# A two-layer kernel whose first layer walks its images in wavefronts: two wavefronts of 8 images against three of 4, 8 and 4

## The chip, the cores and the metric

The kernel runs on one core of one Trainium2 chip. A core has TensorE (PE in the profile, with the loading of its stationary operand shown apart as PEld), VectorE (DVE), ScalarE (ACT), GpSimd (POOL) and SyncE (SP), which here only issues DMAs. ScalarE's own queue issues DMAs too. The metric is the time of one execution on the device in microseconds (us), lower is better; the time given is the median of several executions.

## The reference

The input `x` has 16 images of 64 x 64 positions with 128 channels, in float32. Layer 0 normalises each image by groups of 4 channels (the mean and the variance go over all positions of an image), runs a two-dimensional recurrent cell over it and adds the result to `x`. Layer 1 normalises again, runs a selective scan over the positions forward and backward, and adds that. The change touches layer 0 alone:

```python
def col_step(carry, cols):
    h_l, c_l = carry
    pf0, pf1, pi, po, pc, h_u, c_u = cols          # p* = normalised x @ w* + b*
    f0 = jax.nn.sigmoid(pf0 + h_u @ uf0)
    f1 = jax.nn.sigmoid(pf1 + h_l @ uf1)
    hsum = h_u + h_l
    it = jax.nn.sigmoid(pi + hsum @ ui)
    ot = jax.nn.sigmoid(po + hsum @ uo)
    cp = jnp.tanh(pc + hsum @ uc)
    c = f0 * c_u + f1 * c_l + it * cp
    h = ot * jnp.tanh(c)
    return ((h, c), (h, c))
...
x = x + _L0_conv_ref(_gn(x), ...)
x = x + _L1_conv_ref(_gn(x), ...)
```

A position needs the `h` and `c` of the position above it and of the one to its left. All positions of one anti-diagonal are therefore independent of each other, and a 64 x 64 image has 127 anti-diagonals, with 1, 2, ..., 64, ..., 2, 1 positions.

## The kernel before

**Layer 0 (lines 687 to 853).** Channels lie on the 128 partitions. A wavefront is a set of images that go through their diagonals together: the columns of one step are the positions of the diagonal times the images of the wavefront, so a wavefront of 8 images (`HB`) has 8, 16, ..., 512, ..., 8 columns. There are two wavefronts, images 0 to 7 and 8 to 15.

`statistics(b, q)` (lines 706 to 718) loads a quarter of an image (256 KB, into `xs`, a ring of 4), turns its eight blocks of 128 x 128 with TensorE (line 715) into two PSUM tiles and takes their moments on VectorE (line 716, two instructions); after the fourth quarter line 718 gathers the image's moments. `normal(w)` makes a wavefront's scale and shift from them with `group_norm` (lines 658 to 676): three small matmuls, a few VectorE instructions, a Square and a Sqrt on ScalarE.

One step of a wavefront is three calls. `load(k, w)` (lines 760 to 780) brings the diagonal's positions in by DMAs of up to 128 rows (SyncE's queue, line 767, `xl`, a ring of 8), turns the blocks on TensorE (line 771, `pt`), and applies scale and shift on VectorE (lines 774 and 779, `xn`). `cell` (lines 782 to 814) makes `hs`, the sum of the two neighbours' `h` (line 790), then for each of five gates two matmuls, input weights and recurrent weights (lines 796 and 797), each of which the trace shows as two records; ScalarE takes each gate out of PSUM (line 800); products and sums follow on GpSimd (line 808) and VectorE (809 to 812), one more tanh on ScalarE (813) and the new `h` on VectorE (814). `store` (lines 816 to 831) turns `h` back (line 823, `ph`), adds it to `xl` (lines 826 and 829) and sends the blocks to `x1` by DMAs on ScalarE's queue (line 831).

Buffers: the gates have five PSUM banks (`gate`), the turned blocks and statistics share three (`misc`); the activated gates `a_*` and `hs` have two buffers each, `xn` three.

**The order (lines 833 to 853).** The statistics of the first wavefront's 8 images come first, then `normal(0)`. The second wavefront follows `LATER` diagonals behind the first: the 8 other images have 32 quarters (`rest`), and one quarter is taken at each step, so `LATER` is 34. From then on the steps of the two wavefronts alternate until the first has done its 127 diagonals; the second is alone for the last 34. When the statistics are over, `normal(1)` and the zeroing DMAs of layer 1's `diag` tiles (`clear`, 15 of 256 KB) are issued between steps. At each step the load of the next step is issued ahead of the cell, and the store of the step before behind it. A scheduler orders each engine's instructions from this program; each engine then runs its own list in order, and waits by semaphores.

**Layer 1 (lines 856 on)** starts when layer 0 has let go of its buffers; its order is written out by a planner and is not touched.

Of the kernel before, what the change touches and what calls it, by code (L numbers as in the profile page):

```python
# [8 lines left out]
F32 = mybir.dt.float32  # L9
# [5 lines left out]
P = 128  # L15
B, HH, WW, C = 16, 64, 64, 128
L = HH * WW
# [6 lines left out]
NQ, QP = 2, 64  # L24
# [1 line left out]
NCH = L // T  # L26
PAD = TAPS - 1
NB = T // P
HB = B // 2
GI = P // HB  # L30

# [601 lines left out]
@with_exitstack  # L633
def conv_preact_kernel(ctx: ExitStack, tc: tile.TileContext, a: dict):
    nc = tc.nc
    x, out = a["x"], a["out"]

    const = ctx.enter_context(tc.tile_pool(name="const", bufs=1))
    dram = ctx.enter_context(tc.tile_pool(name="dram", bufs=1, space=DRAM))
    x1 = dram.tile([B * L, C], F32, name="x1")  # L640


    ident = const.tile([P, P], F32, name="ident")
    make_identity(nc, ident)
    eps = const.tile([P, 1], F32, name="eps")
    nc.vector.memset(eps, GN_EPS)

    gavg = const.tile([P, P // GROUP, GROUP], F32, name="gavg")  # L650
    gsum = const.tile([P, P // GROUP], F32, name="gsum")
    nc.vector.tensor_reduce(
        gsum, ident.rearrange("p (g k) -> p g k", k=GROUP), mybir.AxisListType.X, ALU.add
    )
    nc.vector.tensor_scalar_mul(gavg, bc(gsum, 2, GROUP), 1.0 / GROUP)
    gavg = gavg.rearrange("p g k -> p (g k)")

    def group_norm(pool, psum, mv, n, tag, bank="misc"):
# [12 lines left out]
        nc.scalar.activation(std, pv, AF.Sqrt, bias=eps)  # L671
        scale = pool.tile([P, n], F32, name=f"scale_{tag}", tag="gn_scale")
        nc.vector.reciprocal(scale, std)
        shift = pool.tile([P, n], F32, name=f"shift_{tag}", tag="gn_shift")
        nc.vector.scalar_tensor_tensor(shift, mean, -1.0, scale, ALU.mult, ALU.mult)
        return scale, shift


    n = max(sum(k in "NU" for k in kinds) for kinds in KINDS)
    diags = [  # L680
        [dram.tile([P, T], F32, name=f"diag_{i}_{k}") for k in range(n)] for i in range(SETS)
    ]
    layer0(tc, a, const, ident, group_norm, x, x1, sum(diags, []))
    layer1(tc, a, const, ident, group_norm, x1, out, diags)


def layer0(tc, a, const, ident, group_norm, x, x1, clear):
# [3 lines left out]
    nc = tc.nc  # L691
    gates = ["f0", "f1", "i", "o", "c"]
    with ExitStack() as ctx:
        wp = ctx.enter_context(tc.tile_pool(name="l0w", bufs=1))
# [7 lines left out]
        NQ = L // P // SB  # L702
# [25 lines left out]
        norm = {}  # L728

        def normal(w):  # L730
            norm[w] = group_norm(gp, psum, mv[:, w * HB : (w + 1) * HB, :], HB, f"l0_{w}")

        for b in range(HB):
            for q in range(NQ):
                statistics(b, q)
        normal(0)
        rest = [(b, q) for b in range(HB, B) for q in range(NQ)]

        state = {}
        for w in range(2):
            for s in "hc":
                for par in range(2):
                    t = wp.tile([P, HH + 1, HB], F32, name=f"{s}_{w}_{par}")
                    nc.vector.memset(t, 0.0)
                    state[s, w, par] = t

        def rows_of(t, w, k, i, m):

            return bass.AP(
                t.tensor,
                t.offset + w * HB * L * C + i * (WW - 1) * C + k * C,
                [[(WW - 1) * C, m], [L * C, HB], [1, C]],
            )

        def blocks_of(n):
            return [(g, min(GI, n - g * GI)) for g in range(-(-n // GI))]

        def load(k, w):  # L760

            lo, hi = max(0, k - (WW - 1)), min(HH - 1, k)
            n = hi - lo + 1
            nm = f"{k}_{w}"
            xl = xp.tile([P, T // P, C], F32, name=f"xl_{nm}", tag="xl")
            for g, m in blocks_of(n):
                nc.sync.dma_start(xl[: m * HB, g, :], rows_of(x, w, k, lo + g * GI, m))
            pt = psum.tile([P, T], F32, name=f"pt_{nm}", tag="misc")
            for g, m in blocks_of(n):
                r = m * HB  # L770
                nc.tensor.transpose(pt[:, g * P : g * P + r], xl[:r, g, :], ident[:r, :r])
            xn = gp.tile([P, HH, HB], F32, name=f"xn_{nm}", tag="xn", bufs=3)
            xv = xn[:, :n, :]
            nc.vector.tensor_mul(
                xv,
                pt[:, : n * HB].rearrange("p (i b) -> p i b", b=HB),
                bc(norm[w][0], 1, n),
            )
            nc.vector.tensor_add(xv, xv, bc(norm[w][1], 1, n))
            return k, w, lo, n, nm, xl, xv  # L780

        def cell(loaded):

            k, w, lo, n, nm, _, xv = loaded
            cols = n * HB
            hp, cp = state["h", w, (k + 1) % 2], state["c", w, (k + 1) % 2]
            hn, cn = state["h", w, k % 2], state["c", w, k % 2]
            up, left = slice(lo, lo + n), slice(lo + 1, lo + 1 + n)
            hs = gp.tile([P, HH, HB], F32, name=f"hs_{nm}", tag="hs")
            nc.vector.tensor_add(hs[:, :n, :], hp[:, up, :], hp[:, left, :])  # L790
            rec = [hp[:, up, :], hp[:, left, :]] + [hs[:, :n, :]] * 3
            act = []
            for gi, g in enumerate(gates):
                pg = psum.tile([P, T], F32, name=f"pg_{g}_{nm}", tag="gate", bufs=5)
                pgv = pg[:, :cols]
                nc.tensor.matmul(pgv, lhsT=w_sb[:, gi, :], rhs=xv, start=True, stop=False)
                nc.tensor.matmul(pgv, lhsT=u_sb[:, gi, :], rhs=rec[gi], start=False, stop=True)
                ag = gp.tile([P, HH, HB], F32, name=f"a_{g}_{nm}", tag=f"a_{g}")
                agv = ag[:, :n, :]
                nc.scalar.activation(  # L800
                    agv.rearrange("p i b -> p (i b)"),
                    pgv,
                    AF.Tanh if g == "c" else AF.Sigmoid,
                    bias=b_sb[:, gi : gi + 1],
                )
                act.append(agv)
# [9 lines left out]
        def store(loaded):  # L816

            k, w, lo, n, nm, xl, _ = loaded
            hv = state["h", w, k % 2][:, lo + 1 : lo + 1 + n, :].rearrange("p i b -> p (i b)")
            ph = psum.tile([P, T // P, C], F32, name=f"ph_{nm}", tag="misc")  # L820
            for g, m in blocks_of(n):
                r = m * HB
                nc.tensor.transpose(ph[:r, g, :], hv[:, g * P : g * P + r], ident)
            full = n // GI
            if full:
                nc.vector.tensor_add(xl[:, :full, :], ph[:, :full, :], xl[:, :full, :])
            if n % GI:
                r = (n % GI) * HB
                nc.vector.tensor_add(xl[:r, full, :], ph[:r, full, :], xl[:r, full, :])
            for g, m in blocks_of(n):  # L830
                nc.scalar.dma_start(rows_of(x1, w, k, lo + g * GI, m), xl[: m * HB, g, :])

        LATER = len(rest) + 2
        ND = HH + WW - 1
        steps = []
        for t in range(ND + LATER):
            steps += [(t, 0)] * (t < ND) + [(t - LATER, 1)] * (t >= LATER)
        before, now = None, load(*steps[0])
        for n in range(len(steps)):
            if rest:  # L840
                statistics(*rest.pop(0))
            elif 1 not in norm:
                normal(1)
                zeros = xp.tile([P, T], F32, name="zeros", tag="xs", bufs=4)
                nc.vector.memset(zeros, 0.0)
            elif clear:
                nc.sync.dma_start(clear.pop(), zeros)
            after = load(*steps[n + 1]) if n + 1 < len(steps) else None
            cell(now)
            if before:  # L850
                store(before)
            before, now = now, after
# [522 lines left out]
```

## Time and profile before

| what | value |
|---|---|
| median of 3 executions | 13241.79 us (13238.22 to 13249.65) |
| the profiled execution, its own time | 13204.66 us |
| its span | 13202.9 us |
| granted TensorE clock, mean over the span | 0.994 |
| PE busy over the span | 12892.4 us (98%) |
| DVE busy over the span | 12069.2 us (91%) |
| ACT busy over the span | 11514.2 us (87%) |
| first gate matmul of layer 0 starts at | 81.30 us |
| last `h` of layer 0 written at | 1548.56 us |

The profiled execution is 37 us shorter than the median of the others. A span is the time from the first to the last instruction of the profiled execution. Matmuls are pipelined and the ends of their records are modelled, so records overlap and a sum of their durations is more than the time they take: what a matmul costs TensorE is read from the distance of two starts. Issuing a DMA is not counted as busy, though it takes time on the queue of the engine that issues it (ACTq, SPq in a timeline). Layer 0 is the first 1549 us of the span, an eighth of it.

### The profile page before, as it was taken

The page shows a single profiled execution, that of the slowest core. Times are in us where ns is not written, and L with a number is a line of the kernel's source. Part 1 is how long each engine was busy: PE and PEld are TensorE (multiplying, and loading weights), DVE is VectorE, ACT ScalarE, POOL GpSimd, SP SyncE. Part 2 cuts the span into 40 slices and gives each one's busy share as a digit, 9 for nine tenths or more (in the row PEclk, how much of TensorE's full clock was granted, in tenths as well). Part 3 has the DMA queues.
Part 4 walks back from the last instruction along what each step waited for, and adds up shares of the span by engine and source line. Part 5 has one row for each costly group of instructions (what it writes and reads, how often), then busy time and mean ns, then how long its engine had stood idle before and what let it go on. Part 6 is the DMA issues. An engine that isn't in the chain of part 4 may idle for free. (4 is left out here: it accounts for less than half of the span.)

```text
span 13202.9 us, 263832 instructions
## 1 busy us (share of the span) xinstructions
PE 12892.4 (98%) x91444; PEld 10824.2 (82%) x91444; DVE 12069.2 (91%) x14353; ACT 11514.2 (87%) x21184; POOL 11263.7 (85%) x4996
## 2 busy tenths in 40 slices
PE   8999899999999999999999999999999999999999
PEld 7666788888888888888888888888888888888887
DVE  6676599999999999999999999999999999999999
ACT  3444599999999999999999999999999999999998
POOL 0111299999999999999999999999999999999999
PEclk8999999999999999999999999999999999999999
DMA  4221266656666666666566666666565656666665
GB/s 143 54 57 52 62 167 163 171 160 171 164 166 165 165 167 162 170 160 172 158 172 162 167 166 164 166 162 171 159 173 161 168 161 170 164 162 166 163 166 146
DMA packets 2777751, 2025.28 MB, mean 153 GB/s; under 512 B 1584848, under 2 KB 1930464, under 8 KB 2776416
## 3 DMA queue, kind: packets, MB, share of 16 engines
q1 hardware_dynamic: 2698464, 1973.16, 56.9%
q10 hardware_dynamic: 77952, 35.24, 1.1%
q8 instruction: 725, 11.88, 0.4%
q14 instruction: 610, 5.00, 0.1%
HBM read 1849.24 MB, written 157.02 MB: 152 GB/s over the span
## 5 line engine op out<-in xcount | busy, mean ns | idle before, releaser
L1221 POOL TENSOR_TENSOR hc<-hst,cr 128x1024 f32<-128x1024 f32 x3328 | 7802.1, 2377 | 286.9 <-DVE hst L1195 226.2
L1195 DVE TENSOR_TENSOR_SCAN hst<-das,carry,hps 128x512 f32<-128x512 f32 x3808 | 4668.2, 1262 | 184.0 <-PE hps L1183 87.2
L1230 PE MATMUL py<-ident,hc 128*128 128x128 f32 x32768 | 4144.9, 274 | 54.8 <-POOL hc L1221 53.4
L1230 PEld LDWEIGHTS py<-ident,hc 128*128 128x128 f32 x32768 | 3672.2, 141 | 450.2 <-issue 272.0
L1145 ACT ACTIVATE das<-dt,A_log_sb 128x512 f32<-128x512 f32 x5888 | 3875.6, 713 | 121.1 <-DVE hst L1195 79.1
L1157 ACT ACTIVATE dbt<-dtxt,bt 128x256 f32<-128x256 f32 x7680 | 3231.7, 498 | 160.0 <-PE hps L1183 147.6
L1150 POOL TENSOR_TENSOR dbx<-dtx,br 128x1024 f32<-128x1024 f32 x1152 | 2728.6, 2382 | 10.1
L1195 DVE TENSOR_TENSOR_SCAN hst<-da,carry,dbx 128x512 f32<-128x512 f32 x2016 | 2469.2, 1261 | 31.7 <-ACT da L1145 29.9
L1183 PE MATMUL hps<-ident,dbt 128*128 128x128 f32 x15360 | 2261.3, 274 | 104.4 <-DVE hc L1223 80.4
L1174 PE MATMUL hps<-dg,dtxt 128*128 128x128 f32 x16384 | 2176.4, 277 | 37.3 <-DVE hst L1195 20.3
L1183 PEld LDWEIGHTS hps<-ident,dbt 128*128 128x128 f32 x15360 | 1782.0, 141 | 434.0 <-issue 300.4
L1174 PEld LDWEIGHTS hps<-dg,dtxt 128*128 128x128 f32 x16384 | 2005.8, 192 | 117.4 <-DVE hst L1195 46.5
L1014 PE MATMUL pp<-xT,wk 128*128 128x512 f32 x4096 | 1901.6, 596 | 1.9 <-ACT xT L984 1.9
L1195 DVE TENSOR_TENSOR_SCAN hps<-das,carry,hps 128x512 f32<-128x512 f32 x1344 | 1654.7, 1266 | 19.2 <-PE hps L1174 9.6
L1145 ACT ACTIVATE da<-dt,A_log_sb 128x512 f32<-128x512 f32 x2304 | 1556.4, 683 | 80.5 <-DVE hst L1195 59.3
L808 POOL TENSOR_TENSOR a_f<-a_f,c 128x288 f32<-128x288 f32 (+40 forms) x254 | 212.0, 835 | 1332.8 <-ACT a_f L800 1261.9
L1223 DVE TENSOR_TENSOR hc<-hps,cr 128x512 f32<-128x512 f32 x1536 | 1025.7, 674 | 225.8 <-DMA cr<-rows 214.2
L1014 PEld LDWEIGHTS pp<-xT,wk 128*128 128x128 f32 x4096 | 716.5, 190 | 628.9 <-issue 604.0
L1119 POOL TENSOR_TENSOR dtx<-dt,xc 128x1024 f32<-128x1024 f32 x256 | 607.7, 2374 | 296.5 <-ACT dt L1113 225.9
L1195 DVE TENSOR_TENSOR_SCAN hst<-das,hps 128x512 f32<-128x512 f32 x544 | 641.7, 1203 | 83.0 <-issue 27.4
L800 ACT ACTIVATE a_f<-pg_f,b_sb 128x288 f32<-128x288 f32 (+40 forms) x508 | 217.0, 471 | 362.5 <-DMA x<-xl 160.1
L1102 PE MATMUL pv<-dbl,dt_wT 128*128 128x256 f32 x2048 | 507.2, 380 | 8.5 <-ACT xc L1025 8.5
(113 smaller groups left out, 12661.8 us busy)
## 6 DMA issues: line engine op xcount, KB each, us to landing
cr<-rows SPq DMA_DIRECT2D x4096, 256.0 KB
br<-rows SPq DMA_DIRECT2D x1152, 256.0 KB
dg<-diag SPq DMA_DIRECT2D x1024, 256.0 KB
yf<-yo SPq DMA_DIRECT2D x128, 512.0 KB
yl<-yf SPq DMA_DIRECT2D x128, 512.0 KB
carry<-hst SPq DMA_DIRECT2D x3328, 1.0 KB
xs<-in_x_dram SPq DMA_DIRECT2D x64, 512.0 KB
xl<-x SPq DMA_DIRECT2D x128, 256.0 KB
```

The source lines that it names most:

```text
L1014: nc.tensor.matmul(self.ps["conv", h], lhsT=wk[:, k, h * P : (h + 1) * P], rhs=xT[self.b % 2][:, t0 : t0 + T], start=(k == 0), stop=(k == ...
L1102: nc.tensor.matmul(pv[:, q * TQ : (q + 1) * TQ], lhsT=dt_wT[:, q, h * P : (h + 1) * P], rhs=self.dbl, start=True, stop=True,)
L1119: nc.gpsimd.tensor_mul(self.dtx, self.dt, self.xc)
L1145: nc.scalar.activation(t, self.dt[:, h, :], AF.Exp, scale=amat[:, h, s : s + 1])
L1150: nc.gpsimd.tensor_mul(t, self.dtx, bc(self.brow.pop(s), 1, NH))
L1157: nc.scalar.activation(t[:, j, :], self.dtxt[:, j, :], AF.Copy, scale=self.bt[:, j, s : s + 1])
L1174: nc.tensor.matmul(t[:, j * P : (j + 1) * P], lhsT=self.dtxt[:, j, h * P : (h + 1) * P], rhs=self.dbt[s][:, j, :], start=True, stop=True,)
L1183: nc.tensor.transpose(t[:, j * P : (j + 1) * P], self.dbt[s][:, j, h * P : (h + 1) * P], ident)
L1195: nc.vector.tensor_tensor_scan(t[:, self.rev], self.da.pop((s, h))[:, self.rev], dbx[:, self.rev], 0.0 if self.first else carry[:, self.d, ...
L1221: nc.gpsimd.tensor_mul(self.hc[s], self.hst[s], bc(self.crow[s], 1, NH))
L1223: nc.vector.tensor_mul(self.hc[s][:, h, :], self.h[s, h], self.crow[s])
L1230: nc.tensor.matmul(self.py[:, j, cols], start=j not in self.banks, stop=last, skip_group_check=True, **how,)
```

## The change

The two wavefronts of 8 images become three, of 4, 8 and 4 images (`WAVES`), whose first images are 0, 4 and 12. Everything that went by `HB` goes by the wavefront's own number of images `nb`; a block of 128 rows holds 32 positions of a 4-image wavefront and 16 of an 8-image one. The statistics of the first 4 images come ahead of the first diagonal. Those of the other 12 (48 quarters) are taken two at each step of the first wavefront (`PACE`), and `normal(w)` follows as soon as a wavefront's last quarter has been taken. The second wavefront starts 18 diagonals behind the first (32 quarters by two, and two more), the third 26. The rings of `scale` and `shift` get three buffers, since three wavefronts' values live at once. The `clear` DMAs are issued after the last quarter, as before.

```diff
-HB = B // 2
-GI = P // HB
+WAVES = ((0, 4), (4, 8), (12, 4))
...
         def normal(w):
-            norm[w] = group_norm(gp, psum, mv[:, w * HB : (w + 1) * HB, :], HB, f"l0_{w}")
-
-        for b in range(HB):
+            b, nb = WAVES[w]
+            norm[w] = group_norm(gp, psum, mv[:, b : b + nb, :], nb, f"l0_{w}")
+
+        for b in range(WAVES[0][1]):
             for q in range(NQ):
                 statistics(b, q)
         normal(0)
-        rest = [(b, q) for b in range(HB, B) for q in range(NQ)]
+        rest = [(b, q) for b in range(WAVES[0][1], B) for q in range(NQ)]
...
-        LATER = len(rest) + 2
+        PACE = 2
+        later = [0]
+        for b, nb in WAVES[1:]:
+            later.append(-(-(b + nb - WAVES[0][1]) * NQ // PACE) + 2)
         ND = HH + WW - 1
-        steps = []
-        for t in range(ND + LATER):
-            steps += [(t, 0)] * (t < ND) + [(t - LATER, 1)] * (t >= LATER)
+        steps = [
+            (t - d, w)
+            for t in range(ND + later[-1])
+            for w, d in enumerate(later)
+            if 0 <= t - d < ND
+        ]
+        zeros = None
         before, now = None, load(*steps[0])
         for n in range(len(steps)):
-            if rest:
-                statistics(*rest.pop(0))
-            elif 1 not in norm:
-                normal(1)
+            if rest and steps[n][1] == 0:
+                for _ in range(min(PACE, len(rest))):
+                    b, q = rest.pop(0)
+                    statistics(b, q)
+                    for w, (first, nb) in enumerate(WAVES):
+                        if (b, q) == (first + nb - 1, NQ - 1):
+                            normal(w)
+            elif not rest and zeros is None:
                 zeros = xp.tile([P, T], F32, name="zeros", tag="xs", bufs=4)
                 nc.vector.memset(zeros, 0.0)
-            elif clear:
+            elif clear and zeros is not None:
                 nc.sync.dma_start(clear.pop(), zeros)
             after = load(*steps[n + 1]) if n + 1 < len(steps) else None
             cell(now)
```

The rest of the diff puts `nb` for `HB` and `gi = P // nb` for `GI` in `rows_of`, `blocks_of`, `load`, `cell`, `store` and the tiles of `h` and `c`.

More of the change, by code (lines that the diff above doesn't have):

```diff
@@ L671, in group_norm @@
         nc.scalar.activation(std, pv, AF.Sqrt, bias=eps)
-        scale = pool.tile([P, n], F32, name=f"scale_{tag}", tag="gn_scale")
+        scale = pool.tile([P, n], F32, name=f"scale_{tag}", tag="gn_scale", bufs=3)
         nc.vector.reciprocal(scale, std)
-        shift = pool.tile([P, n], F32, name=f"shift_{tag}", tag="gn_shift")
+        shift = pool.tile([P, n], F32, name=f"shift_{tag}", tag="gn_shift", bufs=3)
         nc.vector.scalar_tensor_tensor(shift, mean, -1.0, scale, ALU.mult, ALU.mult)
@@ L736, in layer0 @@
         normal(0)
-        rest = [(b, q) for b in range(HB, B) for q in range(NQ)]
+        rest = [(b, q) for b in range(WAVES[0][1], B) for q in range(NQ)]
         state = {}
-        for w in range(2):
+        for w, (_, nb) in enumerate(WAVES):
             for s in "hc":
                 for par in range(2):
-                    t = wp.tile([P, HH + 1, HB], F32, name=f"{s}_{w}_{par}")
+                    t = wp.tile([P, HH + 1, nb], F32, name=f"{s}_{w}_{par}")
                     nc.vector.memset(t, 0.0)
@@ L749, in rows_of, with blocks_of @@
         def rows_of(t, w, k, i, m):
+            b, nb = WAVES[w]
             return bass.AP(
                 t.tensor,
-                t.offset + w * HB * L * C + i * (WW - 1) * C + k * C,
-                [[(WW - 1) * C, m], [L * C, HB], [1, C]],
-            )
-        def blocks_of(n):
-            return [(g, min(GI, n - g * GI)) for g in range(-(-n // GI))]
+                t.offset + b * L * C + i * (WW - 1) * C + k * C,
+                [[(WW - 1) * C, m], [L * C, nb], [1, C]],
+            )
+        def blocks_of(n, gi):
+            return [(g, min(gi, n - g * gi)) for g in range(-(-n // gi))]
         def load(k, w):
             lo, hi = max(0, k - (WW - 1)), min(HH - 1, k)
-            n = hi - lo + 1
+            n, nb = hi - lo + 1, WAVES[w][1]
+            gi = P // nb
             nm = f"{k}_{w}"
             xl = xp.tile([P, T // P, C], F32, name=f"xl_{nm}", tag="xl")
-            for g, m in blocks_of(n):
-                nc.sync.dma_start(xl[: m * HB, g, :], rows_of(x, w, k, lo + g * GI, m))
+            for g, m in blocks_of(n, gi):
+                nc.sync.dma_start(xl[: m * nb, g, :], rows_of(x, w, k, lo + g * gi, m))
             pt = psum.tile([P, T], F32, name=f"pt_{nm}", tag="misc")
-            for g, m in blocks_of(n):
-                r = m * HB
+            for g, m in blocks_of(n, gi):
+                r = m * nb
                 nc.tensor.transpose(pt[:, g * P : g * P + r], xl[:r, g, :], ident[:r, :r])
-            xn = gp.tile([P, HH, HB], F32, name=f"xn_{nm}", tag="xn", bufs=3)
+            xn = gp.tile([P, HH, nb], F32, name=f"xn_{nm}", tag="xn", bufs=3)
             xv = xn[:, :n, :]
@@ L775, in load @@
                 xv,
-                pt[:, : n * HB].rearrange("p (i b) -> p i b", b=HB),
+                pt[:, : n * nb].rearrange("p (i b) -> p i b", b=nb),
                 bc(norm[w][0], 1, n),
@@ L784, in cell @@
             k, w, lo, n, nm, _, xv = loaded
-            cols = n * HB
+            nb = WAVES[w][1]
+            cols = n * nb
             hp, cp = state["h", w, (k + 1) % 2], state["c", w, (k + 1) % 2]
@@ L788, in cell @@
             up, left = slice(lo, lo + n), slice(lo + 1, lo + 1 + n)
-            hs = gp.tile([P, HH, HB], F32, name=f"hs_{nm}", tag="hs")
+            hs = gp.tile([P, HH, nb], F32, name=f"hs_{nm}", tag="hs")
             nc.vector.tensor_add(hs[:, :n, :], hp[:, up, :], hp[:, left, :])
@@ L797, in cell @@
                 nc.tensor.matmul(pgv, lhsT=u_sb[:, gi, :], rhs=rec[gi], start=False, stop=True)
[L798 removed]
+                ag = gp.tile([P, HH, nb], F32, name=f"a_{g}_{nm}", tag=f"a_{g}")
                 agv = ag[:, :n, :]
@@ L818, in store @@
             k, w, lo, n, nm, xl, _ = loaded
+            nb = WAVES[w][1]
+            gi = P // nb
             hv = state["h", w, k % 2][:, lo + 1 : lo + 1 + n, :].rearrange("p i b -> p (i b)")
             ph = psum.tile([P, T // P, C], F32, name=f"ph_{nm}", tag="misc")
-            for g, m in blocks_of(n):
-                r = m * HB
+            for g, m in blocks_of(n, gi):
+                r = m * nb
                 nc.tensor.transpose(ph[:r, g, :], hv[:, g * P : g * P + r], ident)
-            full = n // GI
+            full = n // gi
@@ L825, in store @@
             if full:
                 nc.vector.tensor_add(xl[:, :full, :], ph[:, :full, :], xl[:, :full, :])
-            if n % GI:
-                r = (n % GI) * HB
+            if n % gi:
+                r = (n % gi) * nb
                 nc.vector.tensor_add(xl[:r, full, :], ph[:r, full, :], xl[:r, full, :])
-            for g, m in blocks_of(n):
-                nc.scalar.dma_start(rows_of(x1, w, k, lo + g * GI, m), xl[: m * HB, g, :])
-        LATER = len(rest) + 2
-        ND = HH + WW - 1
@@ L835, in layer0 @@
-        steps = []
-        for t in range(ND + LATER):
-            steps += [(t, 0)] * (t < ND) + [(t - LATER, 1)] * (t >= LATER)
+            for g, m in blocks_of(n, gi):
+                nc.scalar.dma_start(rows_of(x1, w, k, lo + g * gi, m), xl[: m * nb, g, :])
+        PACE = 2
+        later = [0]
+        for b, nb in WAVES[1:]:
+            later.append(-(-(b + nb - WAVES[0][1]) * NQ // PACE) + 2)
+        ND = HH + WW - 1
+        steps = [
[4 more added lines that the diff above has]
+        ]
```

## The prediction

> **What bounds the kernel now.** Only layer 0 changes, so I read it by stages. I took the busy time by windows first: statistics ahead of the first gate, wavefront 0 alone, both wavefronts, wavefront 1 alone. Columns: window, its length, then busy time and records of PE, PEld, DVE, ACT, POOL, then granted clock, DMA share, GB/s.
>
> ```profile
> 0.00:49.00 49.00, 28.16 (x159) 25.17 (x160) 30.48 (x54) 1.28 (x1) 0.70 (x6) 0.83 0.75 251
> 49.00:81.00 32.00, 19.49 (x118) 16.24 (x117) 20.54 (x40) 2.65 (x4) 0.00 (x0) 0.80 0.73 252
> 81.00:261.00 180.00, 176.27 (x1069) 160.47 (x1067) 126.16 (x400) 71.90 (x214) 17.17 (x35) 0.86 0.43 133
> 261.00:1385.00 1124.00, 1116.45 (x4715) 737.39 (x4716) 783.13 (x1797) 497.43 (x1103) 177.72 (x184) 1.00 0.20 53
> 1385.00:1549.00 164.00, 140.53 (x815) 124.86 (x813) 92.43 (x342) 68.69 (x213) 17.14 (x35) 0.90 0.11 29
> ...
> 30.00:40.00 10.00, 5.96 (x46) 4.90 (x47) 7.08 (x12) 0.00 (x0) 0.00 (x0) 1.00 0.88 312
> ...
> 81.00:133.00 52.00, 52.00 (x245) 49.51 (x244) 22.42 (x87) 13.80 (x49) 2.08 (x8) 0.50 0.29 88
> ...
> 1519.00:1549.00 30.00, 28.59 (x135) 27.63 (x134) 9.72 (x62) 10.91 (x40) 1.55 (x7) 0.50 0.02 6
> ```
>
> The pairs (1124 us) keep PE full at full clock. The clock is half in the first diagonals and the last ones, where steps have few columns. Then the price of a gate matmul, from a timeline of PE: starts, durations, shapes.
>
> ```profile
> 1362.23 0.68 PE L796 MATMUL pg_o<-xn,w_sb 128*128 128x304 f32 x2
> 1362.75 0.67 PE L797 MATMUL pg_o<-hs,u_sb 128*128 128x304 f32 x2
> 1363.26 0.68 PE L796 MATMUL pg_c<-xn,w_sb 128*128 128x304 f32 x2
> ...
> 1364.88 0.40 PE L796 MATMUL pg_f<-xn,w_sb 128*128 128x24 f32 x2
> ...
> 1366.92 0.38 PE L797 MATMUL pg_c<-hs,u_sb 128*128 128x24 f32 x2
> 1367.14 1.24 PE L796 MATMUL pg_f<-xn,w_sb 128*128 128x296 f32 x4
> ```
>
> Two records of 304 columns start 0.515 us apart from the next two: 0.257 a record, 0.00084 us a column. All 20 records of a 24-column step take 1364.88 to 1367.14, 2.26 us: 0.113 a record, not 0.020. So a step costs PE 20 x max(0.113, 0.00084 x columns), flat below 134 columns, plus 0.109 for each 128-wide transpose (eight from 138.28 to 139.16). At half clock the floor doubles:
>
> ```profile
> 97.66 1.95 PE L715 MATMUL ps<-ident,xs 128*128 128x128 f32 x8
> ...
> 101.09 0.61 PE L796 MATMUL pg_o<-xn,w_sb 128*128 128x32 f32 x2
> 101.52 0.61 PE L796 MATMUL pg_c<-xn,w_sb 128*128 128x32 f32 x2
> ```
>
> That is 0.213 a record. Last the in-order engines beside PE:
>
> ```profile
> 300.15 0.47 DVE L774 TENSOR_TENSOR xn<-pt,scale_l 128x320 f32<-128x320 f32 x1
> 304.46 2.13 ACTq L831 DMA_DIRECT2D x<-xl  x3
> 304.54 0.19 DVE L774 TENSOR_TENSOR xn<-pt,scale_l 128x48 f32<-128x48 f32 x1
> 306.64 0.94 ACT L800 ACTIVATE a_f<-pg_f,b_sb 128x320 f32<-128x320 f32 x2 [3.40 <-DMA x<-xl]
> ```
>
> A VectorE instruction has some 0.14 us whatever its columns, and a store's issue holds ScalarE's queue 0.7 us; gates stand behind it.
>
> **The change part by part.**
>
> *Fewer statistics first.* The eighth image's gathering (line 718) ends at 75.27, the fourth's at 43.62 (starts 74.90 and 43.25, 0.37 each). The first gate follows 6.03 later, at 81.30: the small matmuls, a Square, a Sqrt and two table loads of 1.28. So it starts at 43.62 + 6.03 = **49.65**, 31.65 earlier.
>
> *PE work by 4-image steps.* A wavefront of 8: 32 diagonals (n up to 16) at the floor, 32 x 2.26 = 72.3; the others hold 4096 - 272 = 3824 positions x 8 x 0.0168 = 513.9; 586 in all. A wavefront of 4: 66 diagonals at the floor = 149.2; 4096 - 1122 = 2974 x 4 x 0.0168 = 199.8; 349. Two of these in place of one of 8: **+112**. Blocks: 316 each for 8 images, 190 for 4; 64 more, load and store at 0.109: +14. Statistics inside the diagonals: 48 quarters for 32, 16 x 8 x 0.109 = +14, the counterpart of the 31.65.
> So PE's need after the first gate is now 2 x 586.3 + 632 x 2 x 0.109 + 27.9 = 1338 of 1467 us elapsed: 129 lost. It becomes 586.3 + 698.0 + 151.7 + 41.9 = 1478. With the start at 49.65 the need alone ends at 1527.5. **The change wins only if its losses stay under 21 us.** I go through them by stage.
>
> *Wavefront 0 alone, diagonals 0 to 17 (4 to 72 columns), 16 statistics transposes a step.* Half clock: the step from 99.79 to 106.28 (6.49) plus 8 x 0.213 = 8.2. Full clock: the step from 139.24 to 142.87 (3.63, with VectorE near full) plus two moments of 0.69 = 5.0. All cold 148, all warm 90. Before, the clock came at 133, eight steps in. A 4-image step has half the columns, which speaks for later; 16 transposes in a row (3.4 us at half clock) for earlier, since with transposes alone on PE the clock was 1.00 from 30 to 40 us. I take eight cold and ten warm: **116**.
>
> *Diagonals 18 to 25, two wavefronts.* Need 39.6 + 12 x 8 x 0.109 = 50; all cold 8 x 9.4 + 6 x 3.4 = 96. I take **60**, nearer the need, as one step has 76 columns or more.
>
> *Diagonals 26 to 126, three wavefronts.* Need, summed by the prices above: 676 in the wide part (56 to 99), 566 in the two narrow parts. The trace gives what is lost on top: the pairs of diagonals 62 to 104 ran 611.2 us (558.65 to 1169.85) for a need of 597.4, factor 1.023; those of 35 to 54 ran 202.9 for 189.0, 1.075. Narrow diagonals are where the fixed parts count: at diagonal 40 (164, 184 and 60 columns) PE needs 9.2, VectorE about 30 x 0.14 + 408 x 0.0098 = 8.2, ScalarE 18 x 0.16 + 408 x 0.0046 + 5 x 0.7 = 8.3 (starts 0.405 apart at 320 columns, 0.19 at 40). Three engines within a tenth, in fixed order and with two `a_*` buffers, where the slack is only the third wavefront's. I take the measured factors: 676 x 1.023 + 566 x 1.075 = **1300**; bounds 1.02 throughout (1267) and 1.25 in the narrow parts (1400).
>
> *Diagonals 127 to 144, wavefronts 1 and 2.* Need 89.8. In the tail of before the clock went at 1519, between steps of 64 and 56 columns that took 3.3 us, with 0.0168 x 60 / 3.3 = 0.3 of the time streaming. Here a pair takes about 5.0 and gets there when its columns sum to some 100, at diagonal 139. Until then 60.1 x 1.1 = 66; six cold pairs of 40 x 0.213 + 4 x 0.213 = 9.4: 56. **122**; all warm 99.
>
> *Diagonals 145 to 152, wavefront 2 alone (32 to 4 columns).* Cold like 1519 to 1549, where 6.5 steps took 30: 8 x 4.6 = **37**.
>
> *At nothing.* The third `normal` with its table loads lies in wavefront 0's lone stretch, where ScalarE is busy 72 of 180; uncovered some 6. On SP two `xs` loads a step now stand ahead of the `xl` loads; they wait for their ring of 4, two steps back, at 512 KB in 5 to 8 us against 251 GB/s in the first window; uncovered, a quarter's 4.2 us (issued 0.73, first transposed 5.0) a step, up to 75. The 15 clears move, DMA share 0.20. State tiles hold the same bytes. Layer 1 has the same list.
>
> *Sum.* 49.65 + 116 + 60 + 1300 + 122 + 37 = 1685 against 1549: **+136 us** on the profiled execution's 13204.7, whose median neighbours are 37 longer: 13241.8 + 136, about 13375.
>
> [...]
>
> **Rivals.**
> - *The clock stays down longer.* Lone stretch 148, two-wavefront stretch 96, ten cold pairs at the end (+18): 86 more, 13461. For it: 52 us at 0.50 with PE full. Against: the bursts of transposes.
> - *ScalarE or VectorE sets the narrow diagonals.* Factor 1.25: +100, 13475. For it: the 3.40 us idle behind a store's issue. Against: 1.075 with two wavefronts, and a third step now lies between a cell and its successor.
> - *Losses nearly vanish*, since three wavefronts cover every chain: 90 + 52 + 1267 + 99 + 37 + 49.65 = 1595, 13288. Against: nothing covers the clock.
> - *The floor isn't a price* (the other side): a step's 20 short records overlap other wavefronts' work, so that 4-image steps go by columns: 0.0168 x 4 x 4096 x 2 = 551 instead of 698 is 147 less than the forecast, and with the losses of the rival before it 13288 - 147 = 13141. It decides once over two thirds of the 147 and the smaller losses come. Against: in the 24-column step PE never idled between records and still took 0.113.
>
> **How the numbers follow.** Forecast 0.62 (its own range 13320 to 13425), clock 0.10, ScalarE or VectorE 0.10, losses vanish 0.12, no floor 0.06. The range 13285 to 13460 leaves out the floor rival and the far ends of two others. A measurement of this kernel tells 0.2%, 26 us, from no change: faster means under 13215, the floor rival; same takes a slice of the vanishing losses, 0.06; slower the rest.
>
> **What would show it.** In the profile after: first gate near 50 us; 20 records of any step under 134 columns in 2.26 us; clock 0.50 for about 65 us from there; 1300 us from diagonal 26 to 126, PE at 9s; clock 0.50 again for the last 90 us; layer 1's span unchanged within 15 us. I am wrong if short records come closer than 0.11 us, if the clock is up from the first step, or if PE idles by over a tenth in the narrow diagonals.

## The result, and the profile after

The changed kernel takes 13380.33 us (median of 4, 13372.76 to 13384.13) against 13245.72 before: a ratio of 1.0102, 95% interval 1.009 to 1.0114. The forecast was 13375, with a range of 13285 to 13460. In the profiled executions layer 0's last `h` is written at 1693.6 us, against 1548.6 before. What comes after it, layer 1, takes 11682 us against 11654, 28 us more where the forecast allowed 15. A second profile of the same changed kernel, on another chip, has 11648, and the other kernels below have 11643 to 11661, so I take that difference for one of executions or chips and not of the change. The two profiled executions are 173 us apart and the medians 135, since the profiled execution of before was the one that lay 37 us under its median.

The same view by windows as before, at the bounds of the stages: ahead of the first gate, wavefront 0 alone, two wavefronts, three wavefronts (diagonals 26 to 55, 56 to 99, 100 to 126), wavefronts 1 and 2 until the clock falls, and the rest of layer 0. Columns are the window, its length, the busy time and records of PE, PEld, DVE, ACT and POOL, then the granted clock, DMA share and GB/s.

```profile
0.00:51.00 51.00, 28.91 (x151) 24.93 (x151) 29.72 (x60) 4.32 (x5) 0.70 (x6) 0.88 0.73 239
51.00:144.00 93.00, 91.55 (x688) 88.27 (x688) 68.84 (x241) 31.23 (x112) 4.77 (x18) 0.85 0.65 207
144.00:200.00 56.00, 54.88 (x441) 51.86 (x438) 40.23 (x171) 27.56 (x98) 5.95 (x16) 0.94 0.49 165
200.00:507.00 307.00, 305.99 (x2087) 283.59 (x2087) 220.36 (x855) 166.75 (x540) 44.37 (x90) 0.97 0.16 44
507.00:1226.00 719.00, 704.34 (x3307) 520.57 (x3308) 511.83 (x1312) 335.58 (x797) 100.52 (x132) 1.00 0.19 54
1226.00:1537.00 311.00, 307.69 (x1904) 266.61 (x1902) 216.90 (x776) 159.21 (x485) 42.58 (x81) 0.98 0.15 43
1537.00:1605.00 68.00, 67.14 (x572) 64.22 (x571) 47.57 (x234) 38.52 (x154) 10.05 (x25) 1.00 0.13 35
1605.00:1694.00 89.00, 87.60 (x406) 83.33 (x405) 27.60 (x171) 29.25 (x114) 4.66 (x19) 0.50 0.02 6
```

The reader is to see three things. PE is full nearly everywhere: the time was not lost to waiting engines, it went into PE. The clock is up for most of the first lone stretch (0.85, against 0.50 in the 52 us after the first gate of before), and down at the end. And the widest part, where only PE's columns should count, has idle PE time: 704 busy of 719.

The price of a short step, in PE's timeline of the changed kernel:

```profile
1367.71 0.43 PE L799 MATMUL pg_f<-xn,w_sb 128*128 128x64 f32 x2
1367.98 0.39 PE L800 MATMUL pg_f<-h,u_sb 128*128 128x64 f32 x2
...
1369.54 0.39 PE L799 MATMUL pg_c<-xn,w_sb 128*128 128x64 f32 x2
1369.76 0.39 PE L800 MATMUL pg_c<-hs,u_sb 128*128 128x64 f32 x2
1370.10 0.41 PE L828 MATMUL ph<-ident,h 128*128 128x128 f32 x2
```

Each pair of records starts some 0.22 us behind the pair before it, also with two other wavefronts' work on either side: a 64-column step takes as long as one of 24 columns did.

Stage by stage, in us; the column "again" is a second profile of the same kernel, on another chip. "Need" counts the records in the trace, each at max(0.113, 0.00084 x columns) for a gate and 0.109 for a transpose, at full clock.

| stage | forecast | measured | again | need |
|---|---|---|---|---|
| first gate at | 49.65 | 51.2 | 49.1 | |
| wavefront 0 alone, diagonals 0 to 17 | 116 | 93.1 | 86.3 | 76 |
| two wavefronts, 18 to 25 | 60 | 55.9 | 58.6 | 49 |
| three, 26 to 55 | 305 | 306.7 | 306.5 | 283 |
| three, 56 to 99 | 692 | 719.3 | 719.3 | 677 |
| three, 100 to 126 | 304 | 311.3 | 312.0 | 282 |
| two, 127 to 144 | 122 | 117.7 | 117.9 | 90 |
| wavefront 2 alone, 145 to 152 | 37 | 38.4 | 38.4 | 20 |
| last `h` of layer 0 at | 1685 | 1693.6 | 1688.0 | |

### The profile page after: what moved, and what is told of

Read it like the earlier page. It is cut to its first block, busy times and chain, and to the rows that moved or that the text cites. A ratio compares the mean times of both kernels' runs of the same rounds, so it can differ in the third digit from the quotient of the medians.

```text
span 13375.9 us, 272473 instructions
## 1 busy us (share of the span) xinstructions
PE 13062.7 (98%) x94118; PEld 11144.4 (83%) x94118; DVE 12179.4 (91%) x15537; ACT 11664.9 (87%) x21951; POOL 11266.8 (84%) x5123
## 5 line engine op out<-in xcount | busy, mean ns | idle before, releaser
L1247 PE MATMUL py<-ident,hc 128*128 128x128 f32 x32768 | 4146.8, 274 | 58.6 <-POOL hc L1238 57.4
L1212 DVE TENSOR_TENSOR_SCAN hps<-das,carry,hps 128x512 f32<-128x512 f32 x1344 | 1654.4, 1265 | 19.8 <-PE hps L1191 9.8
L811 POOL TENSOR_TENSOR a_f<-a_f,c 128x4 f32<-128x4 f32 (+35 forms) x381 | 212.9, 559 | 1477.0 <-ACT a_f L803 1306.8
L803 ACT ACTIVATE a_f<-pg_f,b_sb 128x4 f32<-128x4 f32 (+35 forms) x762 | 289.0, 400 | 383.4 <-PE pg_f L800 171.0
```

The source lines that it names most:

```text
L1212: nc.vector.tensor_tensor_scan(t[:, self.rev], self.da.pop((s, h))[:, self.rev], dbx[:, self.rev], 0.0 if self.first else carry[:, self.d, ...
L1247: nc.tensor.matmul(self.py[:, j, cols], start=j not in self.banks, stop=last, skip_group_check=True, **how,)
```

## The experiments

Eleven kernels ran on three more chips, each beside the kernel before on the same chip; the kernel before had medians of 13207, 13205 and 13208 us there, some 39 us under the first chip's. So ratios and the stages of the traces are compared, not times across chips. A ratio is to the kernel before. In diffs the changed kernel is the other side, if nothing else is said.

**The changed kernel once more.** No edit.

> The changed kernel itself once more, beside the others on one chip, since chips differ by some tens of us in the time of the same kernel. About 1.010 of the time before; layer 0 ends between 1685 and 1705 us, the lone stretch of 18 diagonals takes some 93 us, or, if the clock there is a matter of chance, up to 125.

13350.29 us, ratio 1.0111 (1.0097 to 1.0125). The stages are in the table; the lone stretch differs most (86 and 93 us), by the clock: 0.94 here, 0.85 there.

**Four wavefronts of 4 images: the suspected cost once more.**

```diff
-WAVES = ((0, 4), (4, 8), (12, 4))
+WAVES = ((0, 4), (4, 4), (8, 4), (12, 4))
```

(and four buffers for `scale` and `shift`)

> Four wavefronts of 4 images, leads 0, 10, 18 and 26, so the same start and the same end as the changed kernel, with the 8-image wavefront split once more. Doubles the suspected cost. Theory (PE's floor): PE's need from the first gate on rises from 1436 to 1562 us without the statistics, so layer 0 ends 115 to 140 us later, about 13505, with all steps under 134 columns at 2.26 us for 20 records. Rival (fixed parts of VectorE and ScalarE): 127 steps more at some 10 x 0.15 us on VectorE, 190 us more, about 13570, and PE idle between steps.

13625.16 us, ratio 1.0318 (1.0304 to 1.0332): twice the loss forecast. Its windows, with the same columns:

```profile
47.00:275.00 228.00, 224.11 (x1489) 214.34 (x1487) 134.25 (x560) 87.24 (x310) 13.81 (x50) 0.76 0.40 128
275.00:664.00 389.00, 376.01 (x2731) 351.32 (x2729) 259.37 (x1124) 203.54 (x724) 53.67 (x120) 0.94 0.13 37
664.00:1373.00 709.00, 704.17 (x4212) 663.93 (x4212) 556.29 (x1752) 375.98 (x1058) 112.85 (x176) 1.00 0.19 54
1373.00:1703.00 330.00, 326.01 (x2457) 307.74 (x2456) 230.40 (x1014) 185.66 (x648) 46.88 (x108) 0.96 0.14 38
1703.00:1959.00 256.00, 254.61 (x1185) 242.09 (x1185) 82.89 (x486) 87.54 (x325) 15.12 (x54) 0.51 0.04 10
```

The records' need is 1603 us against 1477 in the changed kernel, +126, as worked out. But from the first gate to the last `h` it takes 1911.4 against 1642.3, +269. The rest is the clock. Its half-clock time is the sum of 2 x (1 - clock) x length: here 109 + 47 + 0 + 26 + 251 = 433 us; in the changed kernel's windows above, from the first gate on, 28 + 7 + 18 + 0 + 12 + 0 + 89 = 154. If half clock doubles the need (a short gate record starts 0.213 us behind the one before at half clock and 0.112 at full clock, medians of both main profiles), half the difference, 140, is what it added; 126 + 140 = 266. The time that neither explains is 88 us in the changed kernel and 92 here, with 127 steps more, so fixed parts of VectorE and ScalarE did not set the pace: the rival, with 190 us for them, falls, although the time lies nearer its 13570 than the theory's 13505. Where the theory fell short is the clock: it counted the floor alone, 126 us, and with 127 steps more the half-clock time rose by 279 us besides.

By the same count, need, half of the half-clock time and the rest, the kernel before has 1337, 46 and 84 us of its 1467.3 from the first gate to the last `h`, and the changed kernel 1477, 77 and 88 of its 1642.3. So the 145 us by which layer 0 ends later are 140 of need, 31 of half clock and 4 of the rest, less the 30 by which it starts earlier.

**Two wavefronts of 8 images, two quarters a step.**

```diff
-WAVES = ((0, 4), (4, 8), (12, 4))
+WAVES = ((0, 8), (8, 8))
```

> The changed kernel with two wavefronts of 8 images again, the statistics still two quarters a step, so the second wavefront starts 18 diagonals behind the first and not 34. Theory (PE's floor of 0.113 us a record is what three wavefronts pay for): without 4-image steps the work falls back to that of before, and the lone stretches shrink from 34 diagonals to 18. First gate near 81, 18 lone steps in some 82 us, pairs 1220 us of need x 1.037 = 1265, lone tail 74 us as in the rows of before from 1474.84 to 1548.56: layer 0 ends near 1502, that is some 190 us under the changed kernel and 45 under the one before, about 13200. Rival (the split into three is what lets PE run full, and only the pace of the statistics and fixed parts of ScalarE and VectorE cost time): pairs 18 apart run into each other's chains, and the time stays at or over 13245.

13170.30 us, ratio 0.9972 (0.9961 to 0.9982): 37 us under the kernel before, and by ratio some 180 under the changed one. Wavefront 0 alone, the pairs, wavefront 1 alone:

```profile
76.00:162.00 86.00, 82.60 (x645) 78.07 (x645) 68.39 (x228) 32.79 (x111) 6.34 (x18) 0.92 0.69 229
162.00:1430.00 1268.00, 1262.63 (x5550) 874.79 (x5547) 901.28 (x2140) 581.33 (x1311) 182.09 (x219) 1.00 0.20 53
1430.00:1504.00 74.00, 62.37 (x398) 58.94 (x397) 34.48 (x168) 29.80 (x111) 6.23 (x18) 0.79 0.06 16
```

86 for an expected 82, 1268 for 1265, 74 for 74; layer 0 ends at 1504.3 for 1502. The pace of the statistics and the shorter lead, here changed together, are worth having; the 4-image wavefronts are what costs: with the same pace the changed kernel takes 214 us more from first gate to last `h`, 140 of them need, 49 half clock and 25 the rest.

**One quarter a step: the pace alone undone.**

```diff
-        PACE = 2
+        PACE = 1
```

> The three wavefronts with one quarter of statistics a step as before, so leads of 34 and 50 diagonals. Undoes the pace alone. Theory (bursts of 16 transposes bring the clock up in the lone stretch, bursts of 8 do not until the steps have some 64 columns): the first 16 steps or so stay at half clock and take 6.4 us each, 100 us, the next 18 about 3.8; with the same need of PE elsewhere and a longer pair stretch and lone tail layer 0 ends 50 to 100 us later than the changed kernel, near 13420. Rival (the clock came up for another reason, the shorter steps): lone steps at 3.7 us from the second on, and the end within 35 us of the changed kernel.

13396.92 us, ratio 1.0145 (1.0131 to 1.0159), 47 us over the changed kernel on this chip; layer 0 ends at 1743.4 against 1688.0, 55 later, as the theory had it (the 18 lone steps behind the cold ones took 4.5 us each, not 3.8). The lone stretch of 34 diagonals in two windows, and a step in it:

```profile
47.00:162.00 115.00, 115.00 (x540) 109.33 (x539) 50.64 (x197) 30.33 (x109) 4.80 (x18) 0.50 0.29 89
162.00:231.00 69.00, 61.94 (x491) 58.32 (x489) 53.34 (x184) 30.19 (x100) 6.56 (x16) 0.95 0.48 147
...
101.86 1.95 PE L714 MATMUL ps<-ident,xs 128*128 128x128 f32 x8
...
104.87 0.63 PE L799 MATMUL pg_i<-xn,w_sb 128*128 128x40 f32 x2
105.30 0.63 PE L799 MATMUL pg_o<-xn,w_sb 128*128 128x40 f32 x2
```

115 us at half clock, PE full: with eight transposes in a row among such short steps the clock stayed at 0.50, and it came when the steps had some 72 columns, as before the change. In the changed kernel it was up before the steps had 24:

```profile
72.48 2.80 PE L714 MATMUL ps<-ident,xs 128*128 128x128 f32 x12
...
75.79 0.42 PE L799 MATMUL pg_i<-xn,w_sb 128*128 128x20 f32 x2
76.05 0.38 PE L799 MATMUL pg_o<-xn,w_sb 128*128 128x20 f32 x2
```

Twelve transposes in one piece, and the gates behind them start at full clock's 0.23 to 0.26 us a pair. So it was with the pace of two, with pieces of 11 to 16 transposes, that the clock came up early: 1.00 from 75.9 to 127.0 us, where that of one had 0.50.

**The store a step later.** This asks where the wide part's 719 us went. Each step's store, whose first part is PE's transposes of `h`, is put behind the gates of the second step after it and not the first:

```diff
-        before, now = None, load(*steps[0])
+        waiting, now = [], load(*steps[0])
...
+            while waiting and waiting[0][1] == now[1] and waiting[0][0] == now[0] - 2:
+                store(waiting.pop(0))
             cell(now)
-            if before:
-                store(before)
-            before, now = now, after
-        store(before)
+            while len(waiting) > 1:
+                store(waiting.pop(0))
+            waiting.append(now)
+            now = after
+        for one in waiting:
+            store(one)
```

> The changed kernel with each step's store issued one step later, so that the transposes of h follow the gates of the second step behind it and not the first. Theory (in the wide diagonals PE waits in front of the transposes of the 8-image wavefront's h, because only a short 4-image step lies between): the gaps in front of these transposes, 31 us from 507 to 1537 us, go nearly all, 20 to 30 us less, about 13355. Rival (VectorE or ScalarE sets the pace there and PE's gap is only where it shows): the gap moves to the gates, time within 8 us of the changed kernel.

13333.79 us, ratio 1.0092 (1.0079 to 1.0105): by ratio 25 us under the changed kernel, within the theory's 20 to 30, but as the sum of two opposite differences. The wide part went from 719 to 692 us, and the lone stretch from 93 to 125. The two windows:

```profile
50.00:175.00 125.00, 124.18 (x689) 118.83 (x690) 70.27 (x241) 31.28 (x111) 4.77 (x18) 0.61 0.51 155
546.00:1238.00 692.00, 691.91 (x3304) 523.39 (x3304) 507.20 (x1309) 332.66 (x793) 102.16 (x132) 1.00 0.20 56
```

The clock was 0.61 in the lone stretch, against 0.85 and 0.94 in the changed kernel; the new order also split the transposes there, into pieces of at most 10 from 60 to 140 us, where the changed kernel has one of 11 or more in nearly every step. The time of this kernel varies: the five executions went from 13302 to 13348 us, and the profiled one is the longest, with a mean clock of 0.988 over the whole kernel where the two shortest have 0.991 and 0.992. To keep the two apart, the next kernel stores later only from diagonal 26 on (the diff is against the kernel just shown):

```diff
-            while len(waiting) > 1:
+            while len(waiting) > (steps[n][0] + later[steps[n][1]] >= 26):
```

> The changed kernel with the store one step later only from diagonal 26 on, where three wavefronts run; up to there every engine's order is that of the changed kernel. Theory (the wait for the 8-image wavefront's h in front of its transposes): diagonals 26 to 126 take 1297 us as with the later store throughout, against 1337, and the lone stretch 93, not 125: 35 to 42 us under the changed kernel on the same chip. Rival (the store a step later upsets the clock by itself): it stays within 15 us of the changed kernel.

13297.24 us, ratio 1.0072 (1.0059 to 1.0084), 53 under the changed kernel on the same chip by the medians and 33 by the profiled executions; layer 0 ends at 1652.6 against 1688.0, 35 earlier, although its lone stretch took 98 us against 86. Diagonals 26 to 126 took 1295 us for an expected 1297, so the rival falls. The lone stretch and the wide part:

```profile
49.00:146.00 97.00, 95.75 (x683) 92.62 (x684) 68.34 (x240) 31.49 (x112) 4.80 (x18) 0.80 0.63 197
508.00:1200.00 692.00, 691.90 (x3303) 523.21 (x3302) 507.45 (x1310) 332.47 (x793) 102.40 (x132) 1.00 0.20 56
```

What PE waited for in the wide part, in the changed kernel (engine, line, what it waited for: us, times, longest):

```profile
PE ph L828 <- DVE h L817: 11.3, 24, 1.0
PE pg_f L799 <- ACT a_f L803: 2.4, 7, 0.5
```

With the later store the same view has no line. One such wait, in PE's and VectorE's timelines of the changed kernel:

```profile
932.12 0.54 PE L800 MATMUL pg_c<-hs,u_sb 128*128 128x224 f32 x2
933.00 0.63 PE L828 MATMUL ph<-ident,h 128*128 128x128 f32 x4 [0.34 <-DVE h L817]
...
931.14 0.62 DVE L812 TENSOR_TENSOR a_f<-a_f,c 128x224 f32<-128x224 f32 x1 [0.42 <-ACT a_f L803]
931.86 0.39 DVE L814 TENSOR_TENSOR a_f<-a_f,a_f 128x224 f32<-128x224 f32 x1
932.17 0.69 DVE L817 TENSOR_TENSOR h<-a_o,a_c 128x512 f32<-128x512 f32 x1
```

The 8-image step's `h` (512 columns) stands on VectorE behind two instructions of the 4-image step that follows, one of which waits for ScalarE. It is written at 932.86, and PE, done with the short step's gates, can turn it only then: it goes on at 933.00, 0.5 us late (two records of 0.19 after 932.12 end at 932.50). The view of waits shows 0.34 of it: the modelled end of a gate's record lies 0.16 us behind the time at which the next record could start (0.54 against 0.38 us for the two at 932.12), and covers that much of a wait. By starts, the gaps in front of these transposes are 31 us from 507 to 1537; with the later store 0.5. In that kernel the same place has none:

```profile
917.56 0.47 PE L800 MATMUL pg_c<-hs,u_sb 128*128 128x180 f32 x2
917.86 0.60 PE L828 MATMUL ph<-ident,h 128*128 128x128 f32 x4
```

Two wavefronts should need it less, since a full 8-image step lies between:

> Two wavefronts of 8 images by two quarters a step, with the store one step later from diagonal 18 on. Theory (the wait in front of the transposes of h is small where an 8-image step lies between): only the 10 us of gaps in front of them in the run with two wavefronts by two can go, so 4 to 10 us under that run, layer 0 ends near 1497. Rival (the store behind the wrong step costs two wavefronts as much as three): 25 us or more.

Two wavefronts by two with the later store from diagonal 18: 13173.78 us, ratio 0.9972 (0.9962 to 0.9982), nothing won. From diagonal 18 to 126 it took 1268 us, as without. The gaps in front of `ph` fell from some 10 to 1 us, and those in front of the first gates' input matmuls rose from 17 to some 28: the wait moved. The view of waits puts what it sees of it down to ScalarE's gates (4.9 us) and to `xn` (3.2), and only 0.9 to `h`; why these come late with this order was not followed up. The forecast of 4 to 10 us was too much.

**Ten transposes a step at the end.** Can the clock be held over the last 90 us?

```diff
+        FILL = 138
...
+            if steps[n][0] + later[steps[n][1]] >= FILL:
+                pf = psum.tile([P, T], F32, name=f"pf_{n}", tag="misc")
+                for j in range(10):
+                    nc.tensor.transpose(pf[:, (j % 4) * P : (j % 4 + 1) * P], ident, ident)
```

> The changed kernel with ten transposes of the identity into an unused PSUM tile added to every step from diagonal 138 on; nothing reads them, and the result is untouched. Theory (the last 90 us run at half clock because too little streams through PE): the clock stays at 1.00 to within the last few steps; a pair goes from 9.7 us to about 7.2, a lone step from 4.6 to about 3.5, in all 15 to 25 us less, about 13360. Rival (the tail is set by the chain through ScalarE and VectorE, the clock only follows): the 22 steps get longer by 1.1 to 2.1 us each, 20 to 40 us more.

13374.13 us, ratio 1.0127 (1.0113 to 1.014); layer 0 ends at 1714.3, 21 and 26 us behind the two profiles of the changed kernel. The clock held 20 us longer, to 1625 and not 1605, and fell all the same (1.00 from 1592 to 1625, 0.50 from there to 1714). So the theory falls. The rival's numbers came, but not for its reason: from 1625 on PE is busy for all of the 89 us, so that the added transposes at half clock, and no chain through ScalarE and VectorE, make the steps longer. The next kernel puts `w_sb[:, j % 5, :]` in the first `ident`'s place, so that data streams and not zeros:

> As the run with ten transposes of the identity a step from diagonal 138 on, which did not hold the clock, but now of the gates' weights, so that what streams is data and not nearly all zeros. Theory (the clock follows what switches in the array, and zeros do not count): the clock holds from 138 on, a pair takes about 7.3 us and a lone step about 3.6, layer 0 ends 10 to 25 us before that of the changed kernel and 30 to 45 before that with the identity. Rival (transposes as such do not count): the same half clock, 7 us a lone step, some 20 us over the changed kernel.

13379.80 us, ratio 1.0136 (1.012 to 1.0151); layer 0 ends at 1711.9:

```profile
1592.00:1622.00 30.00, 30.00 (x259) 28.26 (x259) 13.13 (x73) 13.95 (x51) 2.25 (x8) 1.00 0.05 15
1622.00:1712.00 90.00, 90.00 (x424) 85.49 (x423) 19.29 (x119) 21.51 (x80) 3.05 (x13) 0.50 0.01 4
```

The same picture, so zeros were not the reason. The rival's numbers came (half clock, 6.9 us a lone step, layer 0 ending 24 us later on the same chip), but its reason, that transposes do not count, does not fit: with them the clock held for three diagonals more, to 1622 and not 1605. A step of a pair took 3.7 us with them while the clock was up; without them it takes 2.7 just before the fall and 4.85 after it. The ten transposes lie in one piece, 1.25 us of a step (the ten from 1606.93 on). Whether the same ten spread over the step, or some more of them, would hold the clock and win time was not tried and stays open.

**A shorter lead still.** Two wavefronts with four quarters a step (lead 10), alone and with the later store. Beside the two wavefronts of 8 in `WAVES`:

```diff
-        PACE = 2
+        PACE = 4
```

> Two wavefronts of 8 images with four quarters a step, so a lead of 10 diagonals. Theory (the lone stretches cost time by what PE doesn't do there, and narrow diagonals by the clock): lone stretch 10 diagonals of some 7 us, VectorE's eight moments in each; need of the pairs 1261 us x 1.03 = 1300; lone tail 10 steps of 4.6 at half clock = 46, and some 10 us more for pairs that are cold before it: layer 0 ends within 12 us of the run with two wavefronts by two, which was at 1504. Rival (any shorter lead pays in proportion, 8 diagonals fewer at either end): 25 to 40 us earlier than that run.

13184.74 us, ratio 0.9981 (0.9973 to 0.999). From first gate to last `h` 1440.0 us, against 1428.2 with a lead of 18: no shorter, and the rival falls. Layer 0 ends at 1523.5, 19 us later and not within 12, because it also began 7 us later; the five kernels that take eight images' statistics first began between 76.1 and 83.5 us, and no reason for that was sought.

> Both together: two wavefronts of 8 images, four quarters a step, the store one step later from diagonal 10 on. If the two are independent, the sum of what each brings against the run with two wavefronts by two: some 5 to 15 us under it, about 0.995 of the time before. If the later store takes the slack that the shorter lead needs, no better than the better one of the two.

13173.46 us, ratio 0.9978 (0.9969 to 0.9987); 1428.3 us from first gate to last `h`. Not better than two wavefronts by two, so the second of the two cases it is: the intervals of all four two-wavefront kernels overlap.

## Why the prediction was right, point by point

The forecast of 13375 met 13380, and the reason given was the right one: PE is full, and a gate record of a short step costs it 0.112 us, with 4 columns as with 128. That the sum came within 5 us is luck. Two of its terms were off by 23 and 37 us, with opposite signs, and the same kernel took 13350 us on another chip.

- *The start*, 49.65: measured 51.2 and 49.1.
- *The work of 4-image steps*, +112 and +14: shown by the trace of after (at full clock the median distance of two gate records is 0.112 us at every width from 4 to 128 columns, 0.116 at 136, 0.156 at 184 and 0.429 at 512, in the trace of before the same from 8 on; 99 in 100 start 0.095 us or more behind the one before) and by four wavefronts, where the need rose by the +126 worked out. Taking the 4-image steps away and leaving the pace brought the time under that of before.
- *The lone stretch*, 116, eight cold steps and ten warm: the first mis-sized step. It has 93 and 86. Half of the difference is the price of a warm step, 5.0: most took 4.2 to 4.5 us, which is the 4.24 that PE needs, so the two moments on VectorE, which made it 5.0, were not what a step waits for. All warm would have been some 79 and not 90. The other half is the clock. The sign named for it, 0.50 for about 65 us from the first gate, did not come: 28 us were at half clock, and 11 in the second profile. The reasons on either side were both named, but the one that decided was weighed too low: with pieces of 11 to 16 transposes the clock was up from the fifth step on, 1.00 for 51 us, in the first profile. With one quarter a step, so with pieces of eight among steps of the same widths, it was at half for 115 us.
- *Three wavefronts*, 1300: the other mis-sized step, 1337. The narrow part up to 55 had the factor 1.082 for 1.075; the wide part had 1.063 for 1.023, and the part from 100 on 1.102 for 1.075. The factors were read from two wavefronts, where an 8-image step is followed by another one. The change puts a short step there, and the transposes of the store wait behind it. This term was missing; with the later store the wide part has 692 us, the forecast's number, and diagonals 26 to 126 have 1295.
- *The narrow parts, three engines within a tenth*: the rival of ScalarE or VectorE did not come. Nor did the wait for `xl`: behind the first gate of the changed kernel the view of waits gives it 1.7 us of TensorE's weight loads in all.
- *`normal`, at nothing*: it did show. The second wavefront's `normal`, which lies in the lone stretch (the third's table loads come at 184 us, with two wavefronts running), has three table loads of 1.28 us on ScalarE, from 127.9 to 132.3, and its step took 6.8 us where its neighbours took 4.5 in the second profile. In the first one the clock fell with it, to 0.50 from 127 to 141 us, and the step took 10.7; that is most of the 7 us between 93 and 86.
- *The end*, 122 and 37: measured 118 and 38, with the clock falling at 1605, where the step's columns sum to 104 as worked out.
- *The losses that vanish* (0.12) and *no floor* (0.06): excluded by the records and the time. The clock rival named the right place and the wrong direction.

## What to carry to other kernels

Before a step is cut into smaller ones to start earlier, read from PE's starts below which width a matmul stops getting cheaper (here a record of 128 columns took 0.112 us, as one of 4 did), and multiply the difference by every step that falls under it: here 112 us of floor, and 31 more of half clock, stood against 32 us of earlier start. The lead and the width are separate choices; keeping the width and halving the lead won 0.3%. And when a new, short step is put between a step and what is queued behind it on the same engine, check whether the result it needs is there by then.

## What was not expected of the hardware

- The granted clock did not go by a step's columns alone. In the changed kernel it was 1.00 from 75.9 to 127.0 us, where the steps of 4 images have 20 columns and up beside 16 transposes; with one quarter a step it was 0.50 from 47 to 162 us, where they have up to some 72 columns beside eight; and from 1605 on, where a pair has 104 columns and fewer and no statistics, it was 0.50 for 89 us. In the narrow parts it fell for a few us at a time: 0.50 from 1489.0 to 1492.4 us and from 1509.5 to 1512.9, and 1.00 in the 17.1 us between. Nor was it the same each time: the same lone stretch, with the same order on PE, had 86, 90, 90, 93 and 98 us in five profiles (clock 0.94 in that of 86, 0.85 in that of 93, 0.80 in that of 98); with another order of PE one had 125, at 0.61. What sets the clock these runs do not show.
- Some 75 of the 7193 gaps between two gate records in the changed kernel are under 0.10 us, down to 0.03, each within one matmul or gate, mostly the first behind transposes. What sets the 0.11 us of the others no run here tests.
- In the kernel with four wavefronts the half clock added about as much (140 us) as the floor itself (126).
- Issuing a store of up to 128 rows holds ScalarE's queue some 0.6 us (the median of 695 issues in the changed kernel; 0.7 in the row that the prediction shows). It was feared as the bound of the narrow diagonals and was not: with 127 steps more, PE's unexplained time went from 88 to 92 us.
